# A four-layer network on one core: the first attention weighs one unit later and takes in three pieces of preparation

## The chip, the cores and the metric

The kernel runs on one core of a Trainium2 chip. The core has a matrix engine (TensorE, PE in the profile), a vector engine (VectorE, DVE), an activation engine (ScalarE, ACT), a general engine (GpSimd, POOL) and a queue that sends for transfers (SyncE, SP). Each engine takes its own instructions in order; engines wait for each other through semaphores. The metric is the time of one execution on the device in microseconds (us). Before the change it was 2339.91 us, the median of three runs (2333.78 to 2342.82).

## The reference

The reference is a network of four layers on an input `x` of 8 sequences, 512 tokens and 128 features, in float32. Each layer does the same outer step with its own attention and its own feed-forward block:

```python
xn = layernorm(x)
s  = attention(xn)
g  = silu(ffn(xn))
x  = x + s * g
```

The change touches the start of layer 0 and prepared values of other blocks:

- Layer 0's attention has 16 heads of 8 features and a sliding window of 64 tokens; a block of 64 queries sees its own and the previous block's 128 keys, with a mask. Softmax over the keys, weighed values, then an output projection.
- Layer 0's feed-forward block has six linear maps whose weights are stored as 4-bit integers: `w = (q / 7.5 - 1) * scale`, plus a low-rank part `lora_b @ lora_a`.
- Layer 1's attention mixes each token with the one before it (`hidden * m + shifted * (1 - m)`) ahead of three projections; its feed-forward block has eight routed experts and two shared ones.
- Layer 3's attention uses per-head scalars (softplus of four parameter rows, a sigmoid of one, and products of them).

## The kernel before, in words

`x` and its normalized form `xn` are kept transposed in on-chip memory, 128 features by 4096 tokens. `network` runs the stages one after another: constants and loads, `layer_norm` over eight tiles of 512 tokens, `l0_attention`, `l0_ffn`, `l1_layer`, and layers 2 and 3.

**Order.** Most of the work is recorded through `in_order(engine)`: what a stage records there keeps the order in which the Python code issues it, on each engine. What is issued directly (`nc.vector...`, `nc.scalar...`) is placed by a scheduler, which may put it earlier than it stands. Three such pieces matter here: `prep.l0_decode` (three vector operations that turn the 4-bit weights `f0_q` into `wt`), `prep.l3_scalars` (layer 3's scalars, 25 vector and activation operations on 128x16 or 128x64 values), which stands after layer 0 in the code but is placed ahead of the first attention, and the constants of `l2.fill` and `l1.fill` on GpSimd. `l1.fill` also issues, in order on ACT, the two transfers of the expert weights (`m1_w13`, `m1_w2`, shown as `m_w`) and ten activations that make the mixing weights `td`, `rest`, `wm`.

**The layer norm.** For each tile: PE centres it (`ps_c`), ACT squares it (`sq`), DVE sums (`var`), GpSimd takes the inverse root (`rstd`), DVE scales (`row`), PE turns it back (`ps_t`), ACT copies it to `xn`.

**The attention.** The work is cut into 64 units: eight sequences (batches) of eight units, a unit being 128 queries and eight of the 16 heads. The loop runs over rounds u. A round holds, in this order:

- `turned(u)`: PE turns the exponentials of unit u, in two tiles of four heads (`tp`), and ACT copies each into `pt`
- in rounds that end a pair of units, `norm`: DVE takes the reciprocal of the sums (`rec`) and scales the output (`o`)
- `scores(u + 3)`: PE multiplies queries and keys (`sc`), DVE scales and masks (`e`) and takes the maximum (`mx`), GpSimd subtracts it
- `out_rows`: PE turns `o` (`tpo`) and ACT copies it (`ot`)
- ACT takes the exponential of unit u + 2
- `weigh(u)`: PE multiplies `pt` with the values (`av`), 16 small products
- after a batch, `finish`: the output projection (`ps_o`), which DVE copies into `s`
- one step of `project` for the next batch: keys (`ps_k`, then four copies `kb`, in turn on DVE and ACT), queries (`ps_q`, copy `q` on ACT), values in two groups (`ps_v`, copies on ACT)

[...] The scores have two tiles of two banks each, the sums `av` one place, and a pool with three banks (`p_t`) serves all the rest: the two tiles of `tp`, `tpo`, `ps_k`, `ps_q`, `ps_v`, `ps_o`. A tile waits until the previous user of its bank has been copied out. From round 32 on, four rounds also carry a step of `l0_low_rank` (`ps_b`, `ps_l`), which adds the low-rank part to `wt`.

Of the kernel before, what the change touches and what calls it, by code (L numbers as in the profile page):

```python
# [9 lines left out]
F32 = mybir.dt.float32  # L10
I32 = mybir.dt.int32
AF = mybir.ActivationFunctionType
# [4 lines left out]
P = 128  # L17
# [232 lines left out]
def l0_attention(net, xn, s_out, p0, w, bias):  # L250
# [6 lines left out]
    with ExitStack() as st:  # L257
# [92 lines left out]
        def turned(u):  # L350

            pts = []
            for g in range(2):
                tp = p_t.tile([P, 4, P], F32, tag="t", name="tp")
                for j in range(4):
                    pe.transpose(tp[:, j, :], e[u][:, 4 * g + j, :], net.ident)
                pt = p3.tile([P, 4, P], F32, tag="pt", name="pt")
                act.copy(pt, tp)
                pts.append(pt)
            return pts  # L360
# [45 lines left out]
        act.activation(e[1], e[1], AF.Exp)  # L406
        todo = iter(())
        for u in range(N + 2):
            if u < N and u % U == 0 and u // U + 1 < B:
                todo = project(u // U + 1)  # L410
            ended = u >= 1 and u <= N and u % 2 == 0
            if u < N:
                pts = turned(u)
            if ended:
                o = norm(u - 1)
            if u + AHEAD < N:
                scores(u + AHEAD)
            if ended:
                out_rows(u - 1, o)
            if u + 2 < N:  # L420
                act.activation(e[u + 2], e[u + 2], AF.Exp)
            if u < N:
                weigh(u, pts)
            if u >= U and u % U == 1:
                finish(u // U - 1)
            next(todo, None)
            if u == 4 * U:
                low = net.prep.l0_low_rank(
                    p0, lambda name: p_t.tile([P, S], F32, tag="t", name=name), pe, dve, act
                )  # L430
            if u > 4 * U and u % U == 6:
                next(low, None)

# [290 lines left out]
class L1Consts:  # L724
    E = 8

    def __init__(self, net, st):
        nc, tc, E = net.nc, net.tc, self.E
        self.net = net
        self.p1 = p1 = st.enter_context(tc.tile_pool(name="a1_c", bufs=1))  # L730
        self.rw = net.load(p1, "m1_r")
        self.eb = p1.tile([P, E], F32, tag="eb", name="eb")
        nc.sync.dma_start(self.eb, net.ins["m1_eb"].partition_broadcast(P))
        self.w = net.load(p1, "a1_w")
        self.par = net.load(p1, "a1_p")
        self.lg = p1.tile([P, NTILE, E], F32, tag="lg", name="lg")

    def fill(self):
        net, nc, p1, E = self.net, self.net.nc, self.p1, self.E
        act = net.in_order(nc.scalar)  # L740
        self.w13 = net.load(p1, "m1_w13", act)
        self.w2 = net.load(p1, "m1_w2", act)

        w, par = self.w, self.par
        self.td = td = p1.tile([P, 1], F32, tag="td", name="td")
        act.activation(td, par[:, 0:1], AF.Exp)
        act.activation(td, td, AF.Copy, scale=-1.0)
        self.tf = par[:, 1:2]
        self.wm = wm = p1.tile([P, 3, 2, P], F32, tag="wm", name="wm")
        self.rest = rest = p1.tile([P, 3], F32, tag="rest", name="rest")  # L750
        act.activation(rest, par[:, 2:5], AF.Identity, scale=-1.0, bias=net.ones[:, 0:1])
        for i in range(3):
            act.activation(wm[:, i, 0, :], w[:, i, :], AF.Copy, scale=par[:, 2 + i : 3 + i])
            act.activation(wm[:, i, 1, :], w[:, i, :], AF.Copy, scale=rest[:, i : i + 1])
        act.activation(w[:, 3, :], w[:, 3, :], AF.Copy, scale=0.5)
# [22 lines left out]
        nc.gpsimd.memset(self.keep[:, :, 0:1], 0.0)  # L778

# [554 lines left out]
class L2Consts:  # L1334
# [4 lines left out]
    def __init__(self, net, st):  # L1339
# [5 lines left out]
        self.p1 = p1 = st.enter_context(tc.tile_pool(name="a2_c", bufs=1))  # L1345
# [1315 lines left out]
class Prepared:  # L2661
# [29 lines left out]
    def l0_decode(self):  # L2691
        nc, wt, qw, sc = self.net.nc, self.f0_wt, self.qw, self.sc
        nc.vector.tensor_copy(wt, qw)
        nc.vector.tensor_scalar(wt, wt, 1.0 / 7.5, -1.0, ALU.mult, ALU.add)
        nc.vector.tensor_tensor(wt, wt, sc, ALU.mult)
# [34 lines left out]
    def l3_scalars(self):  # L2730
# [9 lines left out]
        nc.vector.scalar_tensor_tensor(sp, raw, -1.0, raw, ALU.mult, ALU.min)  # L2740
        nc.scalar.activation(sp, sp, AF.Exp)
        nc.scalar.activation(sp, sp, AF.Ln, bias=net.ones[:, 0:1])
        nc.vector.scalar_tensor_tensor(sp, raw, 0.0, sp, ALU.max, ALU.add)
        sig2, eta2, gam2, nu = (sp[:, i, :] for i in range(4))

        def vec(tag):
            return p1.tile([P, H], F32, tag=tag, name=tag)

        mu, nmu, v_e2, v_0, coef = vec("mu"), vec("nmu"), vec("v_e2"), vec("v_0"), vec("coef")
        nc.scalar.activation(mu, par[:, 0, :], AF.Exp, scale=-1.0)  # L2750
        nc.vector.tensor_scalar(mu, mu, 1.0, None, ALU.add)
        nc.vector.reciprocal(mu, mu)
        nc.vector.tensor_scalar(mu, mu, 1e-4, None, ALU.add)
        nc.vector.tensor_scalar(nmu, mu, -1.0, None, ALU.mult)

        nc.vector.tensor_scalar(v_e2, nmu, 2.0, None, ALU.mult)
        nc.vector.reciprocal(v_e2, v_e2)
        nc.vector.tensor_tensor(v_e2, v_e2, sig2, ALU.mult)
        nc.vector.tensor_tensor(v_0, eta2, gam2, ALU.add)
        nc.vector.tensor_tensor(v_0, v_0, v_e2, ALU.subtract)  # L2760
        nc.vector.tensor_scalar(coef, nu, float(DH), -0.5, ALU.add, ALU.mult)
        nc.vector.tensor_tensor(coef, coef, par[:, 5, :], ALU.mult)


        norm_0 = vec("norm_0")
        nc.vector.tensor_tensor(norm_0[0:64], nu[0:64], v_e2[0:64], ALU.mult)
        nc.vector.tensor_tensor(norm_0[64:128], nu[64:128], v_0[64:128], ALU.mult)
# [3 lines left out]
        nc.vector.scalar_tensor_tensor(cs, coef, -1.0, coef, ALU.mult, ALU.max)  # L2771
        nc.vector.tensor_scalar(cs, cs, 1e-18, 2e-18, ALU.is_lt, ALU.mult)
        nc.vector.tensor_tensor(cs, cs, coef, ALU.add)
        nc.vector.tensor_scalar(ncs, cs, -1.0, None, ALU.mult)
        nc.vector.reciprocal(inv_cs, cs)
        nc.vector.tensor_scalar(g_v, coef, -1.0, -0.5 * DH, ALU.mult, ALU.add)
        nc.vector.tensor_tensor(g_v, g_v, inv_cs, ALU.mult)
        self.scalars = nu, nmu, v_e2, v_0, norm_0, ncs, inv_cs, g_v


def network(tc, ins, out):
    with ExitStack() as ctx:
# [12 lines left out]
        with tc.tile_pool(name="prep_0", bufs=1) as p0:  # L2795
            w0, b0 = net.load(p0, "a0_w"), net.load(p0, "a0_b")
            prep.l0_load(p0)
            net.layer_norm(x, xn)
            prep.l0_decode()
            l2.fill()  # L2800
            l1.fill()
            l0_attention(net, xn, s, p0, w0, b0)
            l0_ffn(net, x, xn, s, l1)
        prep.l3_scalars()
# [85 lines left out]
```

## Time and profile before

| what | us |
|---|---|
| median of the runs | 2339.91 |
| the profiled execution | 2359.42 |
| its span | 2357.7 |
| layer norm, up to the first projection (0 to 29.09) | 29.09 |
| first projection, up to the first scores (29.09 to 40.81) | 11.72 |
| attention, first units (40.81 to 85.91) | 45.10 |
| attention, steady part (85.91 to 284.83) | 198.92 |
| attention, tail (284.83 to 314.00) | 29.17 |
| PE busy | 2186.5 (93%) |
| DVE busy | 1996.3 (85%) |
| ACT busy | 1856.3 (79%) |
| POOL busy | 1576.9 (67%) |

The profile is that of one execution, with its own time; the runs without the profiler are shorter. The page gives busy times, the chain of work that ended last, and groups of instructions; single stretches are read from the timeline (start, duration, engine, line, operation, output and input tiles, and in brackets how long the engine sat idle before it and what ended that wait) and from tables of busy time by stretch. These tables also give the clock that PE was granted, as a share of full speed. Nearly all instructions carry line 83, that of the `in_order` helper, so the tiles' names tell them apart. A row with "x8" holds eight like instructions, with their start and the time to the end of the last.

### The profile page before, as it was taken

The page shows a single profiled execution, that of the slowest core. Times are in us where ns is not written, and L with a number is a line of the kernel's source. Part 1 is how long each engine was busy: PE and PEld are TensorE (multiplying, and loading weights), DVE is VectorE, ACT ScalarE, POOL GpSimd, SP SyncE. Part 2 cuts the span into 40 slices and gives each one's busy share as a digit, 9 for nine tenths or more (in the row PEclk, how much of TensorE's full clock was granted, in tenths as well). Part 3 has the DMA queues.
Part 4 walks back from the last instruction along what each step waited for, and adds up shares of the span by engine and source line. Part 5 has one row for each costly group of instructions (what it writes and reads, how often), then busy time and mean ns, then how long its engine had stood idle before and what let it go on. Part 6 is the DMA issues. An engine that isn't in the chain of part 4 may idle for free.

```text
span 2357.7 us, 48954 instructions
## 1 busy us (share of the span) xinstructions
PE 2186.5 (93%) x17762; PEld 1526.4 (65%) x17762; DVE 1996.3 (85%) x3579; ACT 1856.3 (79%) x3906; POOL 1576.9 (67%) x1414
## 2 busy tenths in 40 slices
PE   6999998899976999878999999999999999999888
PEld 4666676556523666645776777777777777777776
DVE  4777777985676999759999999999999999999656
ACT  4666664564533899848999999999999999999875
POOL 4444435355274788656788788887888878887554
PEclk7999988999997999989999999999999999999999
DMA  4000001013110000043443444334443344433100
GB/s 142 2 2 2 2 1 36 14 50 72 40 46 14 3 16 16 29 134 100 106 104 90 110 114 106 101 91 110 112 109 100 92 110 113 108 97 84 43 1 37
DMA packets 91617, 156.94 MB, mean 67 GB/s; under 512 B 20144, under 2 KB 44464, under 8 KB 91120
## 3 DMA queue, kind: packets, MB, share of 16 engines
q1 hardware_dynamic: 86736, 140.95, 22.9%
q0 software_dynamic: 4352, 8.92, 1.6%
q10 hardware_dynamic: 288, 3.93, 0.4%
q8 instruction: 142, 2.33, 0.4%
q14 instruction: 99, 0.81, 0.1%
HBM read 30.52 MB, written 12.06 MB: 18 GB/s over the span
## 4 chain that ended last, share of the span: by engine, by line
PE 56%; DVE 30%; issue 4%; ACT 4%; POOL 3%; DMA 1%; SPq 1%; another core or an unknown queue 0%; DVEq 0%; ACTq 0%; POOLq 0%
PE sc L83 10%; DVE sc L83 8%; DVE y L83 6%; DVE r L83 6%; PE ps_av L83 6%; PE ps_u L83 5%; PE tp L83 5%; PE ps_kq L83 4%; PE ps_ab L83 3%; PE av L83 3%; PE ps_n L83 2%; DVE mx L83 2%; DVE e L83 2%; PE ps_v L83 2%; PE ps_y L83 1%
## 5 line engine op out<-in xcount | busy, mean ns | idle before, releaser
L83 POOL TENSOR_TENSOR ek<-E,kn 128x512 f32<-128x512 f32 (+3 forms) x512 | 434.4, 871 | 206.3 <-DMA kn<-nr 205.1
L83 PE MATMUL sc<-r 128*128 128x512 f32 (+3 forms) x1024 | 310.2, 446 | 25.2 <-DVE y L83 22.2
L83 POOL TENSOR_TENSOR e<-e,mx 128x1024 f32<-128x1024 f32 x112 | 212.2, 1900 | 180.8 <-DVE mx L83 94.7
L83 POOL TENSOR_TENSOR r<-r,rs 128x1024 f32<-128x1024 f32 x128 | 304.4, 2378 | 23.0 <-DMA rs<-r 20.9
L83 PE MATMUL ps_av<-u,at 128*128 128x128 f32 x2560 | 307.9, 276 | 0.8 <-ACT o L83 0.8
L83 PEld LDWEIGHTS ps_av<-u,at 128*128 128x128 f32 x2560 | 297.3, 193 | 1.1 <-ACT o L83 1.1
L83 ACT ACTIVATE y<-y,mn 128x384 f32<-128x384 f32 (+3 forms) x512 | 288.6, 569 | 4.0 <-DVE mn L83 3.2
L83 PEld LDWEIGHTS sc<-r 128*128 128x128 f32 x1024 | 165.6, 192 | 190.0 <-issue 118.8
L83 DVE SCALAR_TENSOR_TENSOR y<-sc,qn,V 128x512 f32<-128x512 f32 (+3 forms) x512 | 246.5, 544 | 9.1 <-DVE sc L83 0.5
L83 DVE CUSTOM_DVE_ANT_0 y<-y,ps_g,ncs 128x384 f32<-128x384 f32 (+3 forms) x512 | 253.4, 541 | 0.0
L83 PEld LDWEIGHTS tp<-ident,y 128*128 128x128 f32 x1280 | 161.5, 141 | 115.3 <-issue 49.5
L83 ACT ACT_TABLE_LOAD x175 | 224.5, 1283 | 4.0 <-PEq L2879 0.8
L83 PE MATMUL tp<-ident,y 128*128 128x128 f32 x1280 | 203.9, 274 | 3.4 <-ACT o L83 1.4
L83 ACT COPY at<-tp 128x512 f32<-128x512 f32 (+1 forms) x384 | 195.2, 509 | 7.2 <-PE tp L83 4.4
L83 DVE TENSOR_TENSOR sc<-sc,EF 128x1280 f32<-128x1280 f32 x128 | 192.0, 1500 | 4.4
L83 DVE SCALAR_TENSOR_TENSOR sc<-sc,ek 128x1280 f32<-128x1280 f32 x128 | 189.8, 1483 | 6.5 <-issue 5.0
L83 POOL TENSOR_TENSOR s<-s,o 128x512 f32<-128x512 f32 x120 | 154.1, 1284 | 31.6 <-ACT o L83 31.6
L83 ACT ACTIVATE y<-y 128x1280 f32<-128x1280 f32 x128 | 163.4, 1277 | 5.1 <-DVE y L83 4.4
L83 DVE TENSOR_TENSOR r<-sn,ps_kq 128x1024 f32<-128x1024 f32 x128 | 155.3, 1213 | 9.6 <-ACT sq L83 5.1
L83 ACT ACTIVATE sq<-ps_kq 128x1024 f32<-128x1024 f32 x128 | 131.6, 1028 | 32.3 <-PE ps_kq L83 32.3
L83 DVE TENSOR_TENSOR r<-ct,ps_kq 128x1024 f32<-128x1024 f32 x128 | 155.3, 1213 | 0.0
L83 ACT ACTIVATE e<-e 128x1024 f32<-128x1024 f32 x112 | 117.3, 1062 | 40.9 <-POOL e L83 40.5
(465 smaller groups left out, 5023.3 us busy)
## 6 DMA issues: line engine op xcount, KB each, us to landing
rs<-r SPq DMA_DIRECT2D x256, 256.0 KB
kn<-nr SPq DMA_DIRECT2D x512, 64.0 KB
yrows<-yy SPq DMA_DIRECT2D x36, 128.0 KB
ct<-trig SPq DMA_DIRECT2D x16, 256.0 KB
EF<-E SPq DMA_DIRECT2D x16, 256.0 KB
EF<-E SPq DMA_DIRECT2D x16, 192.0 KB
m_w<-m_w ACTq DMA_DIRECT2D x1, 2560.0 KB
x<-x SPq DMA_DIRECT2D x8, 256.0 KB
```

The costliest lines, as they stand in the source:

```text
L83: ins = op(*args, **kwargs)
```

## The change

The change has five parts.

- `weigh` is issued one round later: round u weighs unit u - 1. `norm` and `out_rows` of a pair move with it to odd rounds, `finish` from position 1 of the next batch to position 2, the low-rank steps from position 6 to 5, and the loop has one round more. `pt` comes from a pool with four buffers instead of three.
- The weight decoding (cast, scaling, multiplication by the scales) becomes three single steps in the loop; the multiplication goes from DVE to GpSimd.
- The ten activations for layer 1's mixing weights become six single steps in the loop, through the attention's ACT order.
- Layer 3's scalars, with the load of their parameters, become eight single steps in the loop, through its DVE and ACT orders.
- The expert weights are sent for by SP instead of ACT, and the loads of layer 1 and 2 follow those of layer 0 in SP's queue.

A step is issued in rounds from 8 on at positions 1, 3 and 6, until all seventeen are used up (rounds 9 to 51).

```diff
@@ l0_attention
+        def early():
+            yield from net.prep.l0_decode(dve, pool)
+            yield from l1.mixing(act)
+            yield from net.prep.l3_scalars(dve, act)
+
+        rest = early()
         todo = iter(())
-        for u in range(N + 2):
+        pts = {}
+        for u in range(N + 3):
             if u < N and u % U == 0 and u // U + 1 < B:
                 todo = project(u // U + 1)
-            ended = u >= 1 and u <= N and u % 2 == 0
+            ended = u >= 3 and u % 2 == 1
             if u < N:
-                pts = turned(u)
+                pts[u] = turned(u)
             if ended:
-                o = norm(u - 1)
+                o = norm(u - 2)
             if u + AHEAD < N:
                 scores(u + AHEAD)
             if ended:
-                out_rows(u - 1, o)
+                out_rows(u - 2, o)
             if u + 2 < N:
                 act.activation(e[u + 2], e[u + 2], AF.Exp)
-            if u < N:
-                weigh(u, pts)
-            if u >= U and u % U == 1:
+            if 1 <= u <= N:
+                weigh(u - 1, pts.pop(u - 1))
+            if u >= U and u % U == 2:
                 finish(u // U - 1)
             next(todo, None)
+            if u >= U and u % U in (1, 3, 6):
+                next(rest, None)
...
-            if u > 4 * U and u % U == 6:
+            if u > 4 * U and u % U == 5:
                 next(low, None)
+        for _ in rest:
+            pass
@@ turned
-                pt = p3.tile([P, 4, P], F32, tag="pt", name="pt")
+                pt = p5.tile([P, 4, P], F32, tag="pt", name="pt")
@@ L1Consts.fill
-        act = net.in_order(nc.scalar)
-        self.w13 = net.load(p1, "m1_w13", act)
-        self.w2 = net.load(p1, "m1_w2", act)
+        self.w13 = net.load(p1, "m1_w13")
+        self.w2 = net.load(p1, "m1_w2")
+    def mixing(self, act):
+        ...
+        act.activation(td, par[:, 0:1], AF.Exp)
+        act.activation(td, td, AF.Copy, scale=-1.0)
+        yield
+        ...
+        act.activation(rest, par[:, 2:5], AF.Identity, scale=-1.0, bias=net.ones[:, 0:1])
+        yield
+        for i in range(3):
+            act.activation(wm[:, i, 0, :], w[:, i, :], AF.Copy, scale=par[:, 2 + i : 3 + i])
+            act.activation(wm[:, i, 1, :], w[:, i, :], AF.Copy, scale=rest[:, i : i + 1])
+            yield
+        act.activation(w[:, 3, :], w[:, 3, :], AF.Copy, scale=0.5)
+        yield
@@ Prepared
+    def l0_decode(self, dve, pool):
+        dve.tensor_copy(wt, qw)
+        yield
+        dve.tensor_scalar(wt, wt, 1.0 / 7.5, -1.0, ALU.mult, ALU.add)
+        yield
+        pool.tensor_tensor(wt, wt, sc, ALU.mult)
+        yield
...
-    def l3_scalars(self):
+    def l3_scalars(self, dve, act):
         ...
+        yield
+        dve.scalar_tensor_tensor(sp, raw, -1.0, raw, ALU.mult, ALU.min)
+        act.activation(sp, sp, AF.Exp)
+        act.activation(mu, par[:, 0, :], AF.Exp, scale=-1.0)
+        yield
+        act.activation(sp, sp, AF.Ln, bias=net.ones[:, 0:1])
+        yield
+        dve.scalar_tensor_tensor(sp, raw, 0.0, sp, ALU.max, ALU.add)
...
@@ network
             prep.l0_load(p0)
+            l2.load()
+            l1.load()
             net.layer_norm(x, xn)
-            prep.l0_decode()
             l2.fill()
             l1.fill()
-            l0_attention(net, xn, s, p0, w0, b0)
+            l0_attention(net, xn, s, p0, w0, b0, l1)
             l0_ffn(net, x, xn, s, l1)
-        prep.l3_scalars()
         l1_layer(net, x, xn, s, l1, l2)
```

## The prediction

> **What bounds the kernel now.** I read the page's head and chain first, then busy times by stretch, then the timeline of the first 130 us, and last the granted clock in short stretches.
>
> ```profile
> span 2357.7 us, 48954 instructions
> ...
> PE 56%; DVE 30%; issue 4%; ACT 4%; POOL 3%; DMA 1%; SPq 1%; another core or an unknown queue 0%; DVEq 0%; ACTq 0%; POOLq 0%
> ```
>
> PE carries most of the chain. By stretch (us, then busy time of PE, weight loads, DVE, ACT and POOL, granted clock, DMA): layer norm, first projection, units 0 to 7, steady attention, its tail.
>
> ```profile
> 0.00:29.09 29.09, 18.04 (x96) 16.69 (x96) 13.73 (x29) 10.75 (x17) 17.64 (x65) 0.88 0.55 153
> 29.09:40.81 11.72, 4.52 (x26) 3.15 (x29) 5.07 (x25) 8.21 (x19) 3.67 (x9) 0.83 0.85 336
> 40.81:85.91 45.10, 39.79 (x437) 24.47 (x437) 28.80 (x30) 22.80 (x35) 18.97 (x10) 0.78 0.00 1
> 85.91:284.83 198.92, 190.09 (x2513) 124.79 (x2512) 148.63 (x175) 128.18 (x204) 92.95 (x49) 0.99 0.01 2
> 284.83:314.00 29.17, 27.00 (x318) 19.75 (x318) 13.67 (x22) 14.33 (x24) 9.48 (x5) 0.76 0.01 2
> ```
>
> Steady attention is PE-bound: 190.09 of 198.92 us busy. What can be saved is in the 86 us ahead of it, where PE waits and runs at clocks of 0.78 to 0.88. The timeline of the start (start, duration, instruction, idle before and what ended it):
>
> ```profile
> 18.40 0.56 DVE L2693 CAST wt<-f_q 128x768 f32<-128x768 int32 x1 [1.75 <-DMA f_q<-f_q]
> 28.46 2.09 ACTq L83 DMA_DIRECT2D m_w<-m_w  x2
> 34.50 0.76 ACT L83 ACTIVATE kb<-ps_k,kbias,hm 128x512 f32<-128x512 f32 x1
> 35.27 1.28 ACT L2742 ACT_TABLE_LOAD   x1
> 36.93 1.28 ACT L2750 ACT_TABLE_LOAD   x1
> 40.74 2.01 PE L83 MATMUL sc<-kb,q 32*64 32x512 f32 x16
> ```
>
> The weight decoding holds the layer norm's DVE queue for a DMA; then ACT sends for expert weights, mixes weights and loads two tables before it gives PE its keys. In the steady part PE's only waits are short:
>
> ```profile
> 112.40 0.30 PE L83 MATMUL tpo<-ident,o 128*128 128x128 f32 x1 [0.24 <-DVE o L83]
> ...
> 122.29 1.09 PE L83 MATMUL sc<-kb,q 32*64 32x512 f32 x8
> 123.05 1.06 ACT L83 COPY pt<-tp 128x512 f32<-128x512 f32 x2
> 123.68 1.13 PE L83 MATMUL av<-vw,pt 128*64 128x9 f32 x32 [0.30 <-ACT pt L83]
> 126.78 0.65 PE L83 MATMUL tp<-ident,e 128*128 128x128 f32 x4 [0.48 <-DVE s L83]
> ```
>
> **The change, part by part.** I write S(u) for the start of sc in round u of the attention loop; position 0 is a round with u a multiple of 8. Gains are against the profiled execution, 2359.42 us (span 2357.7), which lies 19.5 above the median of the runs, 2339.91; I subtract the same microseconds from both.
>
> 1. *Decoding out of the layer norm: +3.0.* DVE ends a reduction at 16.65 and stands until 18.40, then casts (0.56) and later scales (0.55). Without both, the third row starts at about 16.9 instead of 18.95. Replayed with the rows' durations (PE's ps_t 0.64, ps_c 1.0 to 1.2, ACT sq 0.60, DVE 0.7 each), the last copy of xn starts at 25.2 instead of 28.46, 3.2 earlier. The half-clock stretch 19.9 to 23.3, which follows PE's 2.4 us wait for that row, should go too. Bounds: 1.8 (the DMA wait alone) to 3.3. The loads that SP now sends after f_q (layer 2's and 1's small ones) are first used past 400 us.
>
> 2. *ACT freed before the first scores: +6.1.* From ps_k (29.09) to sc (40.74) it is 11.65 us. Without the 2.09 us of issuing, the ten mixing steps up to 34.50 and the two tables (2.56), the distances between the same instructions give: kb on DVE 1.17 after ps_k starts, then ACT +0.84, DVE +0.79, ACT +0.84, q +0.66, its end +0.68: 5.0. The second ps_v group (0.94) waits for the fourth kb and ends at 5.4, where sc starts: 6.2 less; with ps_v at half clock (1.65) 5.5 less. Bounds 5.3 and 6.3.
>
> 3. *Units 0 to 2: +4.2.* sc at full clock is 1.09 instead of 2.01, so tp(0) comes 6.8 after sc instead of 7.7. Then PE does tp, sc, ps_k, tp, at half clock as before (1.9 each), without the 1.9 of av(0) between; ps_k and the kb steps behind it come that much sooner, and av(0) fills later time. Replayed, S(3) comes 22.8 after the first sc, where it was 27.3; up to S(8) 0.3 is lost again (point 4). Bounds: 3.5, and 7.9 if the clock stays full.
>
> 4. *Steady rounds: -0.6.* The floor per batch, from starts of neighbouring instructions: tp, sc, av 3.07 a unit, tpo 0.27 four times, ps_k, ps_q, ps_o 0.91 each, the ps_v groups 1.66: 30.0; the batch takes 31.85 (85.92 to 117.76). The 1.8 of waits are tpo for o twice (0.28), av for pt (0.38), tp for a bank (0.7) and 0.13 more. Now av no longer waits for its pt. But the order of the changed program puts tpo in odd rounds, and in position 1 ps_k and both tp tiles hold all three banks, so tpo waits for the copy of the first tp. That copy stands on ACT behind kb, which waits for DVE: S(0) + 1.23 (e) + 1.32 (mx) + 1.21 (kb) + 0.84 (ACT kb) + 0.68 + 0.63 = S(0) + 5.91, the moment at which av started before (117.76 + 5.92 = 123.68). PE is there at S(0) + 4.99: it waits 0.9. ps_o and ps_q now follow each other, and the second half of tp in position 3 waits for q: 0.5. tpo waits 0.3 once. Sum 1.7 against 1.8, period 31.96: the wait has moved, and six batches lose 0.1 each. Bounds -0.5 to +0.5 a batch.
>
> 5. *Seventeen steps in the loop: -1.0.* DVE gets cast 0.56, scaling 0.55 and 22 small operations of 0.11 to 0.25 (about 3.9 in all); ACT 10 mixing steps (2.5 by their spacing), two exponentials (0.48), the logarithm 0.35 and two tables 2.56; POOL one 128x768 multiply between its 0.87 for 128x512 and 1.90 for 128x1024, ahead of a subtraction whose result tp needs two rounds later; SP the load of par, alone in its queue, with two rounds until its use. Cover: DVE has about 8 of 32 us idle per batch, ACT 11, POOL 16. The one new wait, ACT's exponential for DVE's first small operation in round 35, has pt behind it, due a round later. The larger pool for pt adds no instruction. In position 6 four small DVE operations stand ahead of rec, and tpo waits 0.5 more; Ln with its table stands ahead of pt and delays tp about 0.5. All on the path would be 12; nothing, 0. The expert weights go to SP behind 21 issues, about 21 us in; their 11 us of transfer end long before their first use past 410 us.
>
> 6. *Tail: -1.8.* One av more is left when the last sc is through and the clock falls; at half clock it takes 1.72 (299.75 to 303.16). Bounds 0 and 2.4.
>
> 7. *Clock: -3.3.* The clock is decided in stretches of 3.41 us. These are six (all of PE, then tp alone for two of them):
>
> ```profile
> 122.26:125.67 3.41, 3.11 (x43) 1.68 (x43) 2.13 (x3) 2.70 (x4) 1.34 (x1) 1.00 0.00 0
> 125.68:129.09 3.41, 2.86 (x28) 1.43 (x28) 2.79 (x6) 1.61 (x3) 1.90 (x1) 1.00 0.00 0
> 255.38:258.79 3.41, 2.90 (x45) 1.73 (x45) 2.78 (x5) 2.28 (x5) 1.79 (x1) 1.00 0.00 0
> 258.79:262.20 3.41, 3.41 (x15) 2.25 (x13) 1.22 (x1) 1.65 (x3) 1.90 (x1) 0.50 0.02 5
> 296.34:299.75 3.41, 2.48 (x47) 2.12 (x45) 2.55 (x3) 2.42 (x5) 2.23 (x2) 1.00 0.00 0
> ...
> 125.68:129.09 3.41, 1.25 (x8) 0.78 (x7) 0.94 (x2) 1.00 0.00 0
> 255.38:258.79 3.41, 0.66 (x4) 0.42 (x4) 1.06 (x2) 1.00 0.00 0
> ```
>
> The stretch with 2.90 busy is followed by half clock, the one with 2.86 is not: it holds 1.25 of tp, the other 0.66. So full-width matmuls (tp, ps) count, sc less, av little; 255.38 has 1.0 of tp and tpo with 1.09 of sc and falls, 296.34 has 1.4 and no sc and falls. After the change, from S(1) to the next tp lie 3.26 us with only sc, the 0.9 wait, tpo and av, and ps_o no longer follows. A stretch that begins 3.3 to 5.1 us after S(0) holds no more than those two did: 1.8 of 3.41, so about three of six batches, where one falls now. The fall at 258.79 cost S(1) to S(5) 19.2 instead of 17.54, 1.65. Two more: -3.3. Bounds: +1.65 (none) to -18.2 (all six, two stretches each).
>
> [...]
>
> Sum: 3.0 + 6.1 + 4.2 - 0.6 - 1.0 - 1.8 - 3.3 = 6.6. The profile goes to 2352.8, the median to 2333.3.
>
> **The rivals.** *Slower by the clock.* Place: positions 1 and 2. If all six batches fall for two stretches (18.2) and the tpo wait in position 7 drops the clock once a batch as well (6 x 1.65 = 9.9), 28.1 stand where I put 3.3: 2358.1. It is slower than before once dips cost over 9.9. For it: the stretches at 50.58 and 299.75 show that tp, sc and av at half clock do not restore it. Against: a tpo wait of 0.24 never dropped it.
>
> *The start is not won.* f_q and the scale loads now follow x directly; if they delay x, or PE's clock falls at another place of the layer norm, points 1 and 3 shrink to 1.8 and 0: 2339.9. Against: x is issued first, and PE reads tiles 4 to 7 only from 13.4 on.
>
> *No more dips than now and a start at full clock*: 6.6 + 3.3 + 3.7 = 13.6: 2326.3. For it: the first sc comes only 1.6 us after the last busy PE, not 7.2. Against: before tp(0) PE still waits about 3 us.
>
> **How the numbers follow.** Half a per cent, 11.7 us, is about what a measurement of this kernel can tell from no change. My forecast (the start is won, zero to four more dips, 2328 to 2338) has 0.52, nearly all within the bound, 0.06 below 2328.2. The full-clock rival has 0.24 and the cases between it and mine 0.06: all but 0.02 faster. The start not won: 0.06, within. Slower by the clock: 0.12, all of it over the bound. So faster 0.34, within 0.54, slower 0.12. The range 2322 to 2346 takes in the good ends of points 3, 6 and 7 (17.5 gained) and below most of the dips' bound (6 lost).
>
> **What would show it.** DVE without a wait for f_q; the last xn copy near 25 to 26; the first sc near 31.5; tpo in position 1 waiting about 0.9 for ACT pt and tp in position 3 about 0.5 for ACT q; batch period 32.0; table loads near round 38; more half-clock stretches between S(8) and S(57). The prediction is wrong if the period falls by over 0.5, the clock never dips, or stages behind the attention change.

## The result, and the profile after

The changed kernel takes 2353.01 us, the median of 11 runs (2334.55 to 2366.42), beside 2341.20 for the kernel before in the same rounds: a ratio of 1.0061 with a 95% interval of 1.0036 to 1.0086. It is slower, by a little more than the half per cent that counts here; I had forecast 2333.3, faster by 0.3%, within a range of 2322 to 2346.

The profiled execution took 2352.31 us, near the median of its runs. It is 7 us *shorter* than the profiled execution of before, and that comparison misleads. Chips of the same kind differ: on two of the four chips of the experiments the kernel before has a median of 2340, on the two others of 2362 and 2368. The extra time lies in layer 1's routed experts: from the start of the first feed-forward block to layer 2's first scores out of `gkm` the changed kernel took 421 us in one profile and 443 us on one of the longer chips. The profile of before shows 446 there, as on a chip of the longer kind. Up to the end of the attention no such difference shows, and there the two profiles can be laid side by side. All ratios below are to the kernel before on the same chip.

The page's span and chain of the changed kernel:

```profile
span 2350.6 us, 48947 instructions
...
PE 59%; DVE 28%; POOL 5%; ACT 4%; issue 3%; DMA 1%; SPq 0%; POOLq 0%; DVEq 0%; ACTq 0%
```

Busy time by stretch of the changed kernel (us, then PE, weight loads, DVE, ACT, POOL, granted clock, DMA share): layer norm, first projection, units 0 to 7, steady part to S(56), tail.

```profile
0.00:25.94 25.94, 16.50 (x97) 14.99 (x97) 12.96 (x27) 10.74 (x17) 17.64 (x65) 0.93 0.72 217
25.94:31.36 5.42, 3.73 (x18) 2.47 (x18) 1.62 (x2) 2.47 (x4) 3.63 (x9) 1.00 0.99 417
31.36:71.77 40.41, 35.37 (x407) 21.64 (x406) 29.26 (x30) 22.81 (x36) 18.96 (x10) 0.87 0.04 14
71.77:286.30 214.53, 207.52 (x2465) 136.51 (x2464) 157.90 (x195) 132.60 (x216) 94.10 (x50) 0.88 0.01 2
286.30:329.97 43.67, 41.17 (x399) 28.77 (x399) 16.58 (x25) 16.29 (x26) 10.17 (x6) 0.58 0.00 1
```

The last two stretches in the kernel before, S(8) to S(56) and tail:

```profile
85.91:280.91 195.00, 186.67 (x2463) 122.56 (x2462) 144.84 (x171) 126.24 (x201) 91.05 (x48) 0.99 0.01 2
280.91:313.80 32.89, 30.22 (x366) 21.78 (x366) 17.45 (x26) 16.28 (x27) 11.38 (x6) 0.79 0.01 1
```

The start is won. Unit 8's round begins at 71.77 instead of 85.91. Then the steady part to S(56) takes 214.53 us at a mean clock of 0.88, where it took 195.00 at 0.99, and the tail 43.67 at 0.58, where it took 32.89 at 0.79. The attention ends at 329.97 instead of 313.81. PE is busy all the while; it does not wait more (7.0 us in the steady part, 8.3 before), it runs slower.

The timeline of the changed kernel: its start, then the waits of a batch.

```profile
16.82 0.69 DVE L83 TENSOR_TENSOR row<-ps_c,rstd 128x512 f32<-128x512 f32 x1
24.02 1.86 ACT L83 COPY xn<-ps_t 128x512 f32<-128x512 f32 x3 [1.36 <-PE ps_t L83]
25.94 1.12 PE L83 MATMUL ps_k<-xn,a_w 128*128 128x512 f32 x2 [0.68 <-ACT xn L83]
29.67 0.78 ACT L83 ACTIVATE kb<-ps_k,kbias,hm 128x512 f32<-128x512 f32 x1 [0.88 <-DVE kb L83]
31.36 1.11 PE L83 MATMUL sc<-kb,q 32*64 32x512 f32 x16
...
77.60 0.33 PE L83 MATMUL tpo<-ident,o 128*128 128x128 f32 x1 [0.76 <-ACT pt L83]
84.73 0.66 PE L83 MATMUL tp<-ident,e 128*128 128x128 f32 x4 [0.34 <-ACT q L83]
...
202.84 0.30 PE L83 MATMUL tpo<-ident,o 128*128 128x128 f32 x1 [0.24 <-DVE o L83]
```

The third row is scaled at 16.82 without a wait for the weights; the keys are copied without mixing or table loads between; the first scores run at full clock. The three waits stand where the prediction put them: position 1, position 3, position 7. At full clock a batch takes 31.66 us (71.77 to 103.43).

What takes it back are stretches at half clock. Two of them, by clock stretch of 3.41 us (columns as above):

```profile
139.25:142.66 3.41, 2.65 (x45) 1.63 (x41) 3.04 (x5) 2.98 (x5) 1.67 (x1) 1.00 0.01 2
142.66:146.07 3.41, 3.41 (x22) 1.47 (x22) 1.19 (x3) 2.48 (x6) 1.90 (x1) 0.50 0.00 0
...
228.00:231.41 3.41, 3.41 (x51) 2.17 (x49) 2.52 (x5) 2.49 (x5) 1.90 (x1) 1.00 0.01 2
231.41:234.82 3.41, 3.41 (x16) 1.76 (x16) 2.79 (x5) 1.85 (x4) 1.90 (x1) 0.50 0.00 0
...
245.06:248.47 3.41, 3.41 (x40) 1.80 (x36) 1.39 (x2) 1.59 (x2) 0.50 (x1) 0.50 0.00 0
248.47:251.89 3.42, 3.42 (x13) 2.26 (x12) 2.21 (x4) 0.34 (x1) 1.90 (x1) 0.50 0.00 0
251.89:255.30 3.41, 3.41 (x52) 2.27 (x50) 1.61 (x3) 2.71 (x5) 0.00 (x0) 1.00 0.02 5
```

The first fall follows the wait of tpo in position 1, as foreseen. The second follows a stretch in which PE is busy for the whole 3.41 us. Its work was narrow:

```profile
228.38 1.09 PE L83 MATMUL sc<-kb,q 32*64 32x512 f32 x8
229.40 0.33 PE L83 MATMUL tpo<-ident,o 128*128 128x128 f32 x1
229.66 1.11 PE L83 MATMUL av<-vw,pt 128*64 128x9 f32 x32
230.70 0.71 PE L83 MATMUL ps_l<-f_lb,f_la 32*128 32x128 f32 x4
...
246.77 1.88 PE L83 MATMUL av<-vw,pt 128*64 128x9 f32 x32
248.59 2.08 PE L83 MATMUL ps_k<-xn,a_w 128*128 128x512 f32 x2
250.46 1.74 PE L83 MATMUL tp<-ident,e 128*128 128x128 f32 x8
252.12 1.09 PE L83 MATMUL sc<-kb,q 32*64 32x512 f32 x8
```

And it stays at half for six stretches, 20.5 us, through three rounds of tp, sc and av, until ps_k and tp follow each other. Between unit 8 and the end of the attention this profile has six such falls, of 10.2, 3.4, 3.4, 20.5, 34.1 and 20.5 us, 92 in all; before there were two, of 3.4 and 17.1.

**The books.** Each run gives its mean granted clock. Eight of sc take 1.09 us at full clock (139.06) and 1.98 at half (143.72). From this I estimate that a stretch at half clock loses half its length, so (1 - clock) times the span is about what a run loses to the clock where PE sets the pace, and more than it loses elsewhere: 103 us in the changed kernel's runs (clock 0.956). I use this below to part each difference into clock and the rest. The clocks are on record to 0.001, which is 2.3 us, so the parts are good to some 3 us.

### The profile page after: what moved, and what is told of

It is laid out like the page before. It is cut to its first block, busy times and chain, and to the rows that moved or that the text cites. A ratio compares the mean times of both kernels' runs of the same rounds, so it can differ in the third digit from the quotient of the medians.

```text
span 2350.6 us, 48947 instructions
## 1 busy us (share of the span) xinstructions
PE 2206.4 (94%) x17762; PEld 1539.3 (65%) x17762; DVE 2003.5 (85%) x3578; ACT 1855.7 (79%) x3906; POOL 1577.2 (67%) x1415
## 4 chain that ended last, share of the span: by engine, by line
PE 59%; DVE 28%; POOL 5%; ACT 4%; issue 3%; DMA 1%; SPq 0%; POOLq 0%; DVEq 0%; ACTq 0%
PE sc L83 11%; DVE sc L83 7%; PE ps_av L83 6%; DVE r L83 6%; DVE y L83 6%; PE tp L83 5%; PE ps_kq L83 5%; PE ps_u L83 5%; PE av L83 3%; PE ps_ab L83 3%; PE ps_n L83 2%; PE ps_v L83 2%; DVE mx L83 1%; PE ps_p L83 1%; PE ps_y L83 1%
## 5 line engine op out<-in xcount | busy, mean ns | idle before, releaser
L83 DVE TENSOR_REDUCE mx<-e 128x8 f32<-128x1024 f32 (+1 forms) x112 | 136.3, 1217 | 8.1 <-DVE e L83 0.5
```

What stands on the lines that cost most here:

```text
L83: ins = op(*args, **kwargs)
```

## The experiments

The theory after reading the two traces: the weighing order leaves stretches with too little full-width work, the clock falls there, and it comes back late. The rivals: the seventeen steps in the loop, the loads, or the earlier start itself. Where an expectation gives a time, it is for a chip on which the kernel before takes 2340; the ratios are what is compared.

### Order and start apart

*order_alone* is the kernel before with the later weighing and nothing else:

```diff
-            ended = u >= 1 and u <= N and u % 2 == 0
+            ended = u >= 3 and u % 2 == 1
...
-            if u < N:
-                weigh(u, pts)
-            if u >= U and u % U == 1:
+            if 1 <= u <= N:
+                weigh(u - 1, pts.pop(u - 1))
+            if u >= U and u % U == 2:
                 finish(u // U - 1)
...
```

> The kernel before with nothing but the later weighing (norm, out_rows, finish and low-rank positions moved with it, pt in four buffers); decoding, mixing, scalars and loads stay as before. Theory: first sc at 40.7 as before, about 4 us won by unit 8, then 60 us or more at half clock up to the end of the attention, where it was 20; attention over past 330, 2352 to 2364. Rival (steps or loads cost it): 2334 to 2341, no more half clock than before.

*old_order* is the changed kernel with the same lines turned back.

> The changed kernel with the weighing order of the kernel before: round u weighs unit u again, with its norm, out_rows, finish and low-rank positions, and pt in three buffers. The seventeen steps, the loads and the layer norm stay as changed. Theory (the start is won; the new weighing order lets the matrix clock fall in the attention and loses it again): first sc at 31 to 32, attention over at 303 to 306, at most two falls of the clock in the steady rounds, 2328 to 2334. Rival (the steps in the loop or the loads cost it): the attention still ends past 320 and the time stays at 2346 to 2356.

| kernel | ratio, 95% interval | clock of its runs (before) | us over before, of it clock |
|---|---|---|---|
| order_alone | 1.0048, 1.0024 to 1.0071 | 0.9615 (0.966) | +7.4, +10.9 |
| old_order | 1.0084, 1.0060 to 1.0108 | 0.959 (0.966) | +19.5, +17.3 |

The order alone costs some 7 us, though it wins about 4 at the start: theory right in sign, below the 11 I expected. (Its profile, taken in its fastest run, has 30 us at half clock from unit 8 on, where I expected 60 or more.) But the changed kernel with the *old* order is the slowest of the three. That is a miss of my theory, and the trace shows one reason. Timeline of old_order, all engines, position 3 of round 43 and the next:

```profile
244.59 1.90 POOL L83 TENSOR_TENSOR e<-e,mx 128x1024 f32<-128x1024 f32 x1 [5.26 <-ACT vw L83]
244.82 1.69 DVE L83 TENSOR_SCALAR mu<-mu 128x16 f32<-128x16 f32 x1
...
247.35 0.25 DVE L83 RECIPROCAL rec<-av 128x16 f32<-128x16 f32 x1
...
248.07 0.45 PE L83 MATMUL tpo<-ident,o 128*128 128x128 f32 x1 [2.26 <-DVE o L83]
```

An operation on 128x16 values takes 1.69 us, where it took 0.17 in the kernel before. It ends at 246.51, when GpSimd's subtraction ends (246.49). The steps are issued at the end of a round, behind mx; GpSimd starts its subtraction on mx at that moment. So DVE stands, rec and o come late, and PE waits 2.26 us for o. The next stretch is at half clock. Of the seven falls of this profile from unit 8 on, two, with 10 of 72 us, stand behind such a wait.

In the new order the same thing happens. Timeline of after_again (the changed kernel unaltered, described below):

```profile
230.62 1.90 POOL L83 TENSOR_TENSOR e<-e,mx 128x1024 f32<-128x1024 f32 x1 [2.71 <-DVE v L83]
230.66 1.89 DVE L83 TENSOR_SCALAR coef<-sp 128x16 f32<-128x16 f32 x1
...
232.67 0.25 DVE L83 RECIPROCAL rec<-av 128x16 f32<-128x16 f32 x1
...
233.30 0.33 PE L83 MATMUL tpo<-ident,o 128*128 128x128 f32 x1 [2.67 <-DVE o L83]
...
235.11 1.97 PE L83 MATMUL tp<-ident,e 128*128 128x128 f32 x8
```

The clock falls at 233.9. In the first profile of the changed kernel PE was at half clock in this round already, and the wait was hidden.

### The steps

*steps_tail* leaves the three decoding steps in the loop and issues the other fourteen past round 61, where GpSimd has nothing left to subtract. It ran on two chips, the second time beside the changed kernel. *old_order_steps_tail* has the old order as well.

```diff
-            if u >= U and u % U in (1, 3, 6):
+            if u in (U + 1, U + 3, U + 6):
                 next(rest, None)
+            if u > N - AHEAD:
+                for _ in range(3):
+                    next(rest, None)
```

> The changed kernel with only the three decoding steps left in rounds 9, 11 and 14; the other fourteen steps (mixing weights, last layer's scalars) are issued three a round from round 62 on, when no scores are left to compute. Theory (steps: DVE's small operations of the scalars stand behind GpSimd's subtraction, 1.5 to 1.9 us instead of 0.1 to 0.25, push e, mx and tp back and so start the falls from round 35 on): half clock between unit 8 and the end of the attention from 88 down to 25 to 45 us, 2328 to 2338. Rival (order: the later weighing alone makes the falls): 70 to 100 us at half clock as before, 2346 to 2358.

> The same placing of the steps with the weighing order of the kernel before, so that of the change only the start, the loads and the decoding are left in effect. Theory (steps): the steady rounds are those of the kernel before, PE's waits for o of 1.8 to 2.3 us are gone, the attention is over at 300 to 307, 2327 to 2336. Rival (the earlier start itself shifts the rounds so that the clock falls, whatever the steps): the fall of 20 us ahead of unit 8 and those in the steady part stay, 2345 to 2360.

> steps_tail on the chip of the changed kernel. If the steps in the loop matter in the new order as in the old: 6 to 14 us below the changed kernel, ratio to before 0.999 to 1.004. If the falls come from the order alone, within 4 us of the changed kernel, 1.005 to 1.009.

> The changed kernel on the chip of the other three: 1.005 to 1.009 of before.

*steps_between* keeps all seventeen in the loop, each one round later, but issues them inside `scores`, ahead of mx, where GpSimd is as a rule idle:

```diff
             dve.scalar_tensor_tensor(e[u], sc, scale, ...)
+            if due[0]:
+                due[0] = False
+                next(rest, None)
             mx = p5.tile([P, 8], F32, tag="mx", name="mx")
...
             if u >= U and u % U in (1, 3, 6):
-                next(rest, None)
+                due[0] = True
```

> The changed kernel with each of the seventeen steps issued in the middle of the next round's scores, between e and mx, instead of at the end of its round behind mx: DVE then meets GpSimd idle, since its subtraction starts only behind mx. Theory (small operations of DVE wait until GpSimd's subtraction ends): the five long ones (1.5 to 1.9 us) go back to 0.1 to 0.6, no wait of tpo for o over 1.5 us, ratio to before 1.000 to 1.005, 2 to 8 us below the changed kernel. Rival (they are long for another reason): still 1.5 us or more, and no gain.

| kernel | ratio, 95% interval | clock (before) | us over before, of it clock |
|---|---|---|---|
| after_same | 1.0050, 1.0032 to 1.0069 | 0.956 (0.967) | +14.7, +26.4 |
| steps_between, same chip | 1.0014, 0.9987 to 1.0040 | 0.9605 (0.967) | +7.5, +15.5 |
| steps_tail_same, same chip | 1.0004, 0.9984 to 1.0024 | 0.9625 (0.967) | +0.4, +10.6 |
| steps_tail, another chip | 1.0015, 0.9989 to 1.0040 | 0.9585 (0.963) | +0.6, +10.7 |
| old_order_steps_tail, that chip | 0.9995, 0.9975 to 1.0014 | 0.9635 (0.963) | -3.0, -1.3 |

On one chip the steps in the loop cost the changed kernel 14.3 us (2354.5 against 2340.2), and nearly all of it, 15.8, is clock; the rest of the time hardly moves. This rests on the twelve runs of each: the profiles do not show it. That of steps_tail_same, its slowest run, has 97 us at half clock from unit 8 to the end of the attention, that of after_same 95, and that of steps_tail 81, where I had expected 25 to 45. Where the steps are only put out of GpSimd's way, about half of it comes back by the medians (the two intervals overlap). The timeline of steps_between shows that the collision was the cause of the long operations:

```profile
241.87 0.25 DVE L83 RECIPROCAL mu<-mu 128x16 f32<-128x16 f32 x1
242.16 0.17 DVE L83 TENSOR_SCALAR mu<-mu 128x16 f32<-128x16 f32 x1
...
254.15 0.17 DVE L83 TENSOR_SCALAR coef<-sp 128x16 f32<-128x16 f32 x1
```

GpSimd's subtractions run from 238.92 to 240.82, 244.55 to 246.45 and 252.10 to 254.00 here. The same two operations, 1.69 and 1.89 us long in the changed kernel, take 0.17; the cast of the weights goes from 1.85 to 0.55. One operation still meets a subtraction, at 253.46, and takes 0.56.

My expectation for old_order_steps_tail, 2327 to 2336 with 2341 before, was not met: its ratio allows at most 0.25% less than before, 6 us. Its profile has the win (S(8) at 75.8) and reaches the end of the attention at 313.85, where the profile of before has 313.81, with falls of 20.5 and 13.7 us at 269 and 303. Its runs show no more half clock than those of before, however, so the falls of one profile do not explain them all. Why the earlier start is worth so little in the old order is not settled.

### The clock and the width of the work

*filler* adds three transposes that nothing reads ahead of each tpo, into a free part of the sums' bank; *pos1_fill* does so at position 1 alone (`if u % U == 1 and u < N`). *narrow* puts twelve matmuls of 64 columns by 9 in their place. The edit of filler in the loop:

```diff
+            if ended:
+                for _ in range(3):
+                    pe.transpose(spare, net.ident, net.ident)
             if ended:
                 out_rows(u - 2, o)
```

> The changed kernel with three more 128x128 transposes of the identity, which nothing reads, ahead of every tpo: 96 matmuls more, into a free part of the sums' bank. Theory (the clock falls where a stretch of 3.4 us holds too little full-width work; a third of a us more of it in each odd round keeps it up): under 30 us at half clock between unit 8 and the end of the attention, where it was 92, and 2322 to 2334 in spite of the added work. Rival (PE bound by the amount of work, the clock falls for another reason): 96 x 0.13 us less the waits they fill, 5 to 12 us slower, 2358 to 2365.

> The changed kernel with twelve matmuls of 64 columns by 9 ahead of every tpo instead of the three transposes of the filler: about the same time of PE (12 x 0.034 us against 3 x 0.14), but like av in shape. Theory (what keeps the clock up is full-width work): no help, 80 us or more at half clock between unit 8 and the end, 2352 to 2368. Rival (any work of PE, filling its waits, keeps it up): as the filler, 2330 to 2338.

> The changed kernel with three spare transposes ahead of tpo at position 1 alone, where PE waits 0.76 us: 24 matmuls more, no time of their own. Theory A (the falls begin at the place named in the prediction, between position 1 and 2): half clock between unit 8 and the end from 88 to under 45 us, ratio 0.998 to 1.002. Theory B (the falls that begin at position 3, where tp waits for q, and behind ps_l at position 5 weigh more): 65 to 85 us, ratio 1.002 to 1.006.

| kernel | ratio, 95% interval | half clock, unit 8 to the end, in its profile | us over before, of it clock |
|---|---|---|---|
| filler | 0.9965, 0.9940 to 0.9990 | 29 | -6.5, -10.6 |
| narrow | 1.0532, 1.0488 to 1.0577 | 242 | +124.8, +106.7 |
| pos1_fill | 1.0010, 0.9992 to 1.0028 | 39 | +1.8, +9.5 |
| after_again, chip of pos1_fill | 1.0086, 1.0052 to 1.0119 | 64 | +16.7, +34.1 |

> The changed kernel unaltered, on the chip of the other three, to compare them without the difference between chips: ratio to before 1.004 to 1.009, 60 to 100 us at half clock between unit 8 and the end of the attention. Were the ratio within 0.002 of 1, the loss would belong to the chip and not to the change.

Ninety-six useless matmuls take the ratio from 1.0061 to 0.9965. Two batches of filler:

```profile
72.34:104.91 32.57, 31.83 (x421) 21.08 (x420) 25.61 (x29) 20.88 (x34) 16.44 (x9) 1.00 0.01 2
104.91:137.49 32.58, 31.84 (x422) 21.09 (x421) 23.47 (x27) 21.94 (x39) 15.79 (x9) 1.00 0.01 2
```

Each batch takes 0.9 us longer than the changed kernel's at full clock, and the clock stays at 1.00. The same two batches of narrow, and its added matmuls in the timeline:

```profile
76.24:118.17 41.93, 41.44 (x506) 29.01 (x505) 25.79 (x29) 21.36 (x34) 16.93 (x10) 0.87 0.01 2
118.17:165.76 47.59, 47.10 (x506) 32.14 (x505) 23.66 (x27) 22.09 (x38) 15.62 (x9) 0.75 0.00 1
```

```profile
113.92 1.57 PE L83 MATMUL av<-ident 128*64 128x9 f32 x24 [0.15 <-DVE o L83]
115.41 0.33 PE L83 MATMUL tpo<-ident,o 128*128 128x128 f32 x1
```

PE is 99% busy in both batches and the clock falls to 0.87 and 0.75. So a busy PE did not hold the clock here, and the kind of work made the difference: 1.00 in filler, 0.75 in narrow. The twelve took 1.57 us a round instead of the 0.4 I had expected, so narrow also adds some 6 us of work a batch at full clock, 46 in all, part of it in PE's waits; but 107 of its 125 us are the clock's. Position 1 alone, the place the prediction named, gives back 15 of the 17 us that the changed kernel loses on that chip, with 24 matmuls: theory A, in half clock and in ratio. The falls behind it are still there (27 us from 242 on, in the round of the step that waits longest), and filler, which thickens all odd rounds, is better by another half per cent. The profiles give position 1 less: of the 15 falls in three profiles of the changed kernel two follow its wait, in that of steps_between four of five. Which falls come differs between profiles of the same kernel, and three are too few to weigh the places.

### Orders that keep the clock

*tpo_late* issues tpo behind av. *even_plain* also moves the output projection to position 6 and the steps to the end; it adds no work.

```diff
-            if ended:
-                out_rows(u - 2, o)
...
             if 1 <= u <= N:
                 weigh(u - 1, pts.pop(u - 1))
+            if ended:
+                out_rows(u - 2, o)
-            if u >= U and u % U == 2:
-                finish(u // U - 1)
+            if u >= U and u % U == 6 or u == N + 2:
+                finish(min(u, N) // U - 1)
...
```

*held* is the changed kernel with the steps at the end, the filler, three transposes in every round past 61, and 22 between the first scores and the first tp. *even* is even_plain with those 22, and three at the end of position 1, of position 5 from round 37 on, and of every round past 61. *even_steps_in* is even with the steps back in the loop.

> The changed kernel with tpo issued behind av in its round instead of ahead of it, so that at position 1 it no longer waits for the copy of pt. Theory (little full-width work, at positions 3 to 6 too): the waits of 0.76 and 0.24 us go, the period at full clock falls to 30.7 to 31.2, but the stretches at positions 3 to 6 still drop the clock: 40 to 80 us at half clock, 2338 to 2350. Rival (the wait at position 1 alone is what drops the clock): under 20 us at half clock, 2322 to 2330.

> The changed kernel with three things moved and no work added: tpo behind av, the output projection ps_o at position 6 of the next batch instead of position 2 (away from ps_q, into the thin rounds), fourteen of the steps past round 61. Theory (what counts is full-width work per 3.4 us stretch): waits at positions 1, 3 and 7 nearly gone, full-clock period 30.4 to 31.0, half clock between unit 8 and the end of the attention 20 to 50 us, a ratio to before of 0.990 to 0.998. Rival (weighing later is itself what drops the clock): 70 us or more at half clock, ratio above 1.000.

> A version meant to keep the clock up throughout: the changed kernel with the steps at the end as in steps_tail, three spare transposes ahead of every tpo and in every round past 61, and 22 of them between the first three scores and the first tp, where PE waits 3.2 us. Theory (full-width work): the stretch of 10 us at half clock after 36.9 goes and units 0 to 7 take 4 us less, falls in the steady part under 10 us, 2312 to 2324. Rival (falls come from elsewhere): not below the 2334 of the filler.

> The same with spare transposes: 22 between the first scores and the first tp, three at the end of position 1, of position 5 from round 37 on, and of every round past 61. Theory: no half clock between the start of the attention and its last ten us except by chance, attention over at 293 to 299, ratio 0.988 to 0.993, better than both the kernel before and every other run so far. Rival (the falls elsewhere, or the added work, take it back): 0.995 or above.

> The kernel called even with its seventeen steps back in the loop, in rounds 9 to 51. If the steps stop PE often enough to drop the clock: 5 to 14 us more than even, ratio 0.991 to 0.996, and waits of 1.5 us or more in rounds 40 to 51. If not: 0.987 to 0.990.

| kernel | ratio, 95% interval | end of the attention in its profile | us over before, of it clock |
|---|---|---|---|
| tpo_late | 1.0023, 1.0000 to 1.0045 | 325.8 | +5.9, +16.7 |
| even_plain | 0.9979, 0.9954 to 1.0005 | 312.4 | -2.1, +18.8 |
| held | 0.9957, 0.9933 to 0.9981 | 305.3 | -10.8, -16.9 |
| even | 0.9883, 0.9861 to 0.9904 | 289.6 | -29.7, -22.0 |
| even_steps_in | 0.9939, 0.9915 to 0.9962 | 311.5 | -8.7, -0.3 |

tpo_late brings the period to 31.07 and still loses it to the clock, as expected. even_plain has hardly a wait left (30.33 a batch at full clock), and in most of its runs the clock takes that back too: fewer waits with the same narrow rounds do not hold it. even does, in its four runs (2331 to 2334, where before has 2362 on that chip). held lands between its two expectations: on a chip of 2340 its ratio makes 2330. Busy time of even by stretch: units 0 to 7, steady part to S(56), tail.

```profile
31.38:67.54 36.16, 33.78 (x432) 22.26 (x431) 29.06 (x30) 22.06 (x35) 18.96 (x10) 1.00 0.03 12
67.54:255.47 187.93, 185.14 (x2490) 124.06 (x2489) 146.82 (x173) 124.67 (x202) 92.94 (x49) 0.99 0.01 2
255.47:289.57 34.10, 31.10 (x420) 22.49 (x419) 18.38 (x35) 20.18 (x42) 11.38 (x6) 0.90 0.01 1
```

At 0.9883 it beats both kernels, with some 70 spare transposes in it. Against it, even_steps_in loses half of the gain again, with a wait of 1.85 us for o at 224 and 34 us at half clock behind it. (The two ran on different chips.)

## Why the prediction was wrong, point by point

1. *Decoding out of the layer norm, +3.0*: right. ps_k starts at 25.94 instead of 29.09, 3.15 earlier; the wait for f_q and the half-clock stretch at 19.9 are gone.
2. *ACT freed, +6.1*: right. From ps_k to sc 5.42 instead of 11.65, 6.2.
3. *Units 0 to 2, +4.2*: right. S(3) comes 22.3 after the first sc (I had 22.8). Steps 1 to 3 together: 14.1 by unit 8, where I had 13.3. This refutes the rival "start not won" for the trace.
4. *Steady rounds, -0.6*: right in mechanism, the waits being 0.76, 0.34 and 0.24 us where I had 0.9, 0.5 and 0.3. The size has a slip: my floor of 30.0 and waits of 1.7 make 31.7, not the 31.96 that I wrote. The period is 31.66, where it was 31.85, so at full clock the rounds gain 0.2 a batch.
5. *Seventeen steps, -1.0*: **wrong**. I priced 22 small operations of DVE from their rows of before (0.11 to 0.25 us), where GpSimd was not subtracting beside them. In the loop six of DVE's operations (the cast and five small ones) take 1.5 to 1.9 us, they stand ahead of rec, tpo waits up to 2.7 us, and the clock falls. Measured: 14.3 us on one chip, by putting fourteen of the steps at the end. Even my worst bound, 12, was too small, since it counted the operations' time and not what a stopped PE does to the clock. That the collision makes these operations long is shown by steps_between; that it makes all of the 14.3 us is not: steps_between gets back only about half, and in steps_tail the steps of ACT moved as well. The profile of before had the evidence. There an operation on 128x128 values of wt takes 1.28 us beside GpSimd's subtraction and 0.29 without:

```profile
277.53 1.90 POOL L83 TENSOR_TENSOR e<-e,mx 128x1024 f32<-128x1024 f32 x1 [1.18 <-PE tp L83]
278.23 1.28 DVE L83 TENSOR_SCALAR wt<-wt,mean 128x128 f32<-128x128 f32 x1
...
307.55 0.29 DVE L83 TENSOR_SCALAR wt<-wt,mean 128x128 f32<-128x128 f32 x1
```

I had not set these rows against the new place of the operations. There the scalings of mu and coef took 1.69 us (old_order) and 1.89 (after_again) and ended within 0.03 us of GpSimd's 1.90.
6. *Tail, -1.8*: about right; from the last scores to the feed-forward block 20.7 instead of 18.5 us.
7. *Clock, -3.3*: **wrong**, mis-sized, and only in part in the right place: behind tpo's wait in position 1 the clock does fall (142.66, for 10.2 us), and three transposes there give back 15 of 17 us (pos1_fill). I charged one stretch of 3.41 us, 1.65 us, to each of two more falls. The three profiles of the changed kernel (the first, after_again, after_same) have 15 falls between unit 8 and the end of the attention, four to six each, of 3.4 to 61.4 us, 17 us on average: 8.5 us lost each, five times my price. Most begin where I had not looked. Two, with 17 of the 256 us, follow tpo's wait in position 1; five of one stretch each stand behind position 3, where tp waits for q; one of 10 stands behind the step in round 47, and two with 41 in the tail. The longest, five with 171 us, begin behind the narrow ps_l of position 5 in rounds 45 and 53 (one of them behind a step's wait as well). The change had moved ps_l there from position 6, and I priced that at nothing; no run tests it apart. Without the steps' part the clock costs 10.6 us more than before (steps_tail_same).

On the chip of after_same the sum closes, as it must by the way the parts are taken: 13.3 us more for step 5, 7.3 more for step 7 and 0.7 for all others make 21.3, the distance from the predicted gain of 6.6 to the measured loss of 14.7. The shares are those of one order of removal and do not add up in another: with position 1 filled and the steps left in, pos1_fill also gets nearly all of it back; why the two overlap was not shown. The test in it is the last part: what I summed for the steps other than 5 and 7, 10.9, was measured as 10.2 in steps_tail_same.

The rival "slower by the clock" (2358.1) was the right one, 5 us from the median. Half of its mechanism was right: rounds of tp, sc and av that do not bring the clock back (20.5 us at half clock from 231.41). Its place, positions 1 and 2, was right for a few of the falls, and it had no steps in it, so that its number came so close is in part luck. It had the evidence too: the fall of 17.1 us in the tail of before was five stretches long, and I had priced a fall at one. I gave it 0.12. The collision behind step 5 was in none of the rivals. (The rival "the start is not won" has a slip too: with 1.8 and 0 for points 1 and 3 the sum is 1.2 and the time 2338.7, not 2339.9; and the good ends of points 3, 6 and 7 make 17.05, not 17.5.)

PE's busy share did not tell where the clock fell: in the kernel before, 255.38 to 258.79 is 85% busy, in the changed kernel 228.00 to 231.41 is wholly busy, narrow is 99% busy, and all three were followed by half clock. Nor did the first fall keep its place in the program: it begins at 13.03 us in the profile of before, at 12.96 in the first of the changed kernel, and at 12.0 to 14.1 in sixteen of the eighteen; in the other two, narrow and even_plain, the clock stays full until 35.

## What to carry to other kernels

Where PE's work is partly narrow, price a wait by what it does to the clock, not by its own length: waits of under 1 us were followed by falls that cost 2 to 10 us here, the longer ones where the rounds that followed did not bring the clock back. Look for the rounds with little full-width work. To spread that work more evenly was not enough by itself here (even_plain, 0.9979); a few spare transposes were worth more than they cost (filler, 0.9965; even, 0.9883). And price an operation that is moved by what will run beside it in its new place; on DVE that was GpSimd, and its time grew tenfold, from 0.17 us to 1.69 and 1.89.

## What the runs showed of the hardware

- **The clock went with full-width work.** Counted for each stretch of 3.41 us between the first scores and the end of the attention, in the profile of before and the first of the changed kernel: the busy time of tp, tpo, ps_b and the projections, added up. At full clock, the ten stretches with half clock behind them held 0.00 to 1.39 us of it, the 117 with full clock behind them 1.04 to 2.75. At half clock, the 29 that half clock followed held 0.00 to 2.39, the nine that full clock followed 2.32 to 3.66. A round of tp, sc and av has 1.09 us of it in 3.1 at full clock, and a short wait or a narrow ps_l leaves less in a stretch: 139.25 to 142.66 holds 0.79, 228.00 to 231.41 holds 0.86, and half clock follows both. At half clock such rounds gave 1.86 in 231.41 to 234.82 and none at all in 245.06 to 248.47, and the clock stayed at half; in 248.47 to 251.89, with ps_k and tp behind each other, it was 3.51, and full clock followed. This is a count over two profiles, not a mechanism that was shown.
- **DVE's small operations stood behind GpSimd.** Additions, products and scalings of 128x16 values in on-chip memory that started while GpSimd's 1.90 us subtraction ran ended with it: 1.69 us (old_order) and 1.89 (after_again) where it had just begun, 0.56 where it was nearly over (steps_between); issued ahead of mx, on which the subtraction waits, they took 0.17 (steps_between). Not every operation stood: DVE's own scaling of the scores, out of PSUM (sc), kept its 1.22 us beside it, and so did reductions out of on-chip memory, mx with 1.22 and the mean of wt with 0.29 (before and the changed kernel).
- **The same kernel varies by 1% from run to run, and the clock goes with it.** The changed kernel's first 11 runs go from 2334.55 at a clock of 0.966 to 2366.42 at 0.950: 32 us in time, 39 by the books. In the profiles of before and of the changed kernel the times at one clock, up to the last, are whole multiples of 3.41 us (3.41 to 191.15 in the attention of before). The place of this grid against the program differs from run to run (12.0 to 14.1 us for the first half-clock stretch), and with it which work falls into one stretch. Where two profiles lay alike, so did their falls: the changed kernel and steps_tail both fell at 142.7, 187, 221, 231.4 and 272.4, and steps_tail_same within 0.2 us of these, although fourteen steps had been moved; the last of these falls was 34.1, 30.7 and 61.4 us long.
